# A graph-attention layer and a quantile layer: start-up loads on POOL's queue, shared gather rounds, and the quantile mean on ScalarE and TensorE

## The chip, the cores and the metric

The kernel runs on one core of a Trainium2 chip. The metric is the device time of one execution in microseconds (us). A core has five engines that each work through their own instruction stream in order: TensorE (PE in the profile, its weight loads PEld), VectorE (DVE), ScalarE (ACT), GpSimd (POOL) and SyncE (SP, which here only issues transfers). Engines wait for one another by semaphores. A DMA is issued from the stream of an engine, in order with that engine's other instructions.

## The reference

4096 nodes with 128 features, and a symmetric 4096 x 4096 adjacency matrix with ones on the diagonal, about one entry in 64 set. Layer 0 is graph attention with 8 heads:

```python
Wh = einsum('nd,hde->hne', nodes, W)
f1 = einsum('hnd,hd->hn', Wh, a1); f2 = einsum('hnd,hd->hn', Wh, a2)
e = leaky_relu(f1[:, :, None] + f2[:, None, :], 0.2)
att = softmax(where(adj > 0, e, -9e15), axis=-1)
h = elu(einsum('hnm,hmd->hnd', att, Wh))
x = elu(transpose(h, (1, 0, 2)).reshape(N, 8 * 128) @ W1 + b1)
out = layernorm(nodes + x, gamma, beta)
```

Layer 1 has an adjacency list per node, thinned: of the node's neighbours in order, those whose rank plus one is a multiple of half their number are removed. For each feature, the values of the kept neighbours are sorted, and the values at the ranks of the quantiles 0.25, 0.5 and 0.75 are averaged:

```python
svals = sort(where(keep[:, :, None], x[None], big), axis=1)
for q in (0.25, 0.5, 0.75):
    idx = maximum(ceil(q * n_keep) - 1, 0)
    agg = agg + (1/3) * take_along_axis(svals, idx)
agg = 0.5 * agg + 0.5 * x
out = agg @ W.T + b + x
```

## The kernel before

Line numbers are those of the kernel before, which are also those in its profile. The layers are sparse: neighbours are fetched as rows by indirect DMA (one instruction fetches 128 rows of 512 or 544 bytes, one for each partition, by a list of 128 row numbers). The program (`gnn`) is `gat`, then `sparse`. A second path (`general`) would be taken for graphs that do not fit the sizes assumed, and is not executed here.

**The front (class `Front`).** Nodes are taken in tiles of 128, and tiles in blocks of 4, 4, 6, 6, 6, 6. `scan` loads a tile's adjacency rows in four quarters of 512 KB on SP's queue (three buffers), ACT makes zeros and ones of them (L371, L378), and PE packs 16 columns into a word (L380), into `ps_words`. From the second pair of tiles on, two tiles are scanned together. `first` (L393 and the helper `drain8`, L186 and L188) drains the nonzero words on DVE, 8 a round in 13 rounds; `second` unpacks the bits; another drain puts each node's neighbour list in order. When a block's tiles are through, `place` sorts its nodes by number of neighbours: it computes each node's place in the block (`pos_i`, L509), and 4 or 6 indirect scatters on POOL (L530) write the lists to the DRAM array `rows_d` in that order. `keep` thins the lists for layer 1 (`meta_d`), and after the last block `order` computes each node's place in a global order by number of kept neighbours, which 32 scatters (`scatter`, L669) write to `order_d`. These steps are a list of `pieces`; `advance(n)` puts the next n of them into the program.

**The table.** `table` (L228) loads W, a1, a2 and x, forms W·a for the heads, transposes x on PE, with copies on ACT, and writes a table `xf_d` to DRAM: a row of 128 features, 8 values f2 and 8 values f1 for each node, and a padding row. Twelve DMAs, all from ACT's queue. `gat` then loads the weights, bias, gamma and beta, and writes two padding rows of the table of layer 1, whose source is set by DVE (L817): seven DMAs more from ACT's queue.

**The attention.** The work is cut in 64 units, each half a tile. In a unit, 4 groups of 16 nodes each have an upper bound on their neighbours (nodes being sorted, `BOUNDS` gives it), and a group is fetched in r rounds; in a round, a gather (L890) fetches 8 neighbours for each of the 16 nodes. r is the bound plus 2, over 8, rounded up, so a last round is partly padding. `load(u)` issues these gathers on POOL three units ahead, into six `nb` buffers of 18 rounds. Row numbers come from `ids`, which SP loads from `rows_d` once for a block, with `info`, which the gathers `me` (L866) and the scatters of results (L1098) need. DVE adds f1 and f2 (L966), ACT and DVE form the softmax numerators, DVE spreads them (L1005), and PE multiplies one 128 x 128 matrix per round into `ps_z` (L1012). A framework schedules the instructions of each engine: the order in which they lie in the built program follows dependences and its own estimates, unless `issue_after` ties them, so it is not always the order of the source.

**The quantile stage.** `sparse` (L1570) takes the 32 tiles of the global order. For each it gathers as many rows as the tile's largest list (L1607, POOL; three row buffers), and runs a sorting network over the slots: a step copies the low side on ACT into a PSUM bank or a small buffer (L1645), then DVE takes minimum and maximum (L1650, L1651). Two tiles are interleaved. `quantile` then knows, for each of three quantiles, a short range of sorted slots in which the node's rank lies. DVE forms 0 or 1/3 weights for them (L1684) and sums the weighted slots in `agg`: one L1695 and several L1698 a tile. Where a list is longer than 64, the slots above are merged in by `cut` operations (L1665, L1675, L1680). For a group of up to four tiles, `finish` then has four items: PE adds half of `agg` and half of x, transposed (L1711, L1712); ACT copies that (L1716); PE applies the layer (L1722 to L1724); ACT copies the result (L1728), and POOL scatters it to the output (L1732). Such items wait in a list, from which `compare` takes one a step: a "copy" item after any ACT copy of the network, a "bank" item only in steps with 5 to 12 slots, in the free end of that step's PSUM bank. There are two banks.

## Time and profile before

| | us |
| --- | --- |
| median of 3 runs | 7742.63 (7739.80 to 7743.64) |
| the profiled execution, whole | 7742.94 |
| its span | 7741.1 |
| end of the first block's places (`pos_i`) | 170.2 |
| first neighbour gather | 179.9 |
| first compare of the quantile stage on DVE | 3269 |
| last DVE instruction | 7727.0 |
| mean granted TensorE clock | 0.553 |

The profile is of one execution. Its parts are busy time by engine, the span in 40 slices of 193.5 us with each engine's busy tenths, groups of instructions (line, engine, operation, tiles, shapes and count, then busy time, the mean of one in ns, and the idle time just before them on their engine with what ended it), waits, and a timeline. "issue" in the idle column is time in which an engine waited for nothing that the profile shows. DMA instructions on POOL show the time that POOL spends on them, not that of the transfer.

### The profile page before, as it was taken

The page shows a single profiled execution, that of the slowest core. Times are in us where ns is not written, and L with a number is a line of the kernel's source. Part 1 is how long each engine was busy: PE and PEld are TensorE (multiplying, and loading weights), DVE is VectorE, ACT ScalarE, POOL GpSimd, SP SyncE. Part 2 cuts the span into 40 slices and gives each one's busy share as a digit, 9 for nine tenths or more (in the row PEclk, how much of TensorE's full clock was granted, in tenths as well). Part 3 has the DMA queues.
Part 4 walks back from the last instruction along what each step waited for, and adds up shares of the span by engine and source line. Part 5 has one row for each costly group of instructions (what it writes and reads, how often), then busy time and mean ns, then how long its engine had stood idle before and what let it go on. Part 6 is the DMA issues. An engine that isn't in the chain of part 4 may idle for free. (4 is left out here: it accounts for less than half of the span.)

```text
span 7741.1 us, 30455 instructions
## 1 busy us (share of the span) xinstructions
PE 1051.4 (14%) x5811; PEld 887.8 (11%) x5811; DVE 5841.9 (75%) x9358; ACT 2162.5 (28%) x2127; POOL 4386.7 (57%) x4564
## 2 busy tenths in 40 slices
PE   3233242332232223200000000000000000000000
PEld 1122232222232222100000000000000000000000
DVE  6456465564332222289999999999999999999999
ACT  5021112000000000133333333333333333333332
POOL 0777777777777777575545636354635534554400
PEclk5566666665566666655555555555555555555555
DMA  5232324222222222111111101011101101111100
GB/s 183 67 100 78 97 78 113 64 60 56 47 56 56 56 56 56 41 48 37 35 32 36 42 24 43 27 38 31 45 23 36 36 27 29 37 36 31 31 3 1
DMA packets 222435, 385.05 MB, mean 50 GB/s; under 512 B 121622, under 2 KB 133274, under 8 KB 222234
## 3 DMA queue, kind: packets, MB, share of 16 engines
q0 software_dynamic: 145664, 305.55, 15.4%
q1 hardware_dynamic: 64258, 70.19, 3.0%
q10 hardware_dynamic: 12312, 7.28, 0.3%
q14 instruction: 154, 1.26, 0.1%
q8 instruction: 47, 0.77, 0.0%
HBM read 372.41 MB, written 10.31 MB: 49 GB/s over the span
## 5 line engine op out<-in xcount | busy, mean ns | idle before, releaser
L1607 POOL DMA_INDIRECT rows<-x_d,info x2078 | 2022.4, 973 | 1962.4 <-DVE agg L1698 1272.7
L890 POOL DMA_INDIRECT nb<-xf_d,ids x2250 | 2140.2, 951 | 697.0 <-issue 652.8
L1645 ACT COPY low<-rows 128x2048 f32<-128x2048 f32 (+8 forms) x1022 | 1561.3, 1533 | 2599.7 <-DVE rows L1651 1964.0
L1650 DVE TENSOR_TENSOR rows<-low,rows 128x2048 f32<-128x2048 f32 (+8 forms) x1022 | 1883.1, 1861 | 114.5 <-ACT low L1645 33.8
L1651 DVE TENSOR_TENSOR rows<-low,rows 128x2048 f32<-128x2048 f32 (+8 forms) x1022 | 1881.7, 1860 | 4.7
L966 DVE TENSOR_TENSOR e<-nb,ps_small 128x144 f32<-128x144 f32 (+8 forms) x166 | 43.5, 264 | 1314.1 <-DMA nb<-xf_d,ids 1246.9
L1012 PE MATMUL ps_z<-spread,nb 128*128 128x128 f32 x4500 | 612.1, 304 | 770.2 <-DVE spread L1005 749.0
L1012 PEld LDWEIGHTS ps_z<-spread,nb 128*128 128x128 f32 x4500 | 601.0, 219 | 804.5 <-DVE spread L1005 367.3
L1711 PE MATMUL low<-half_i,agg 128*128 128x128 f32 x64 | 22.2, 451 | 4297.1 <-ACT low L1645 4191.2
L974 ACT ACTIVATE ps_e<-e 128x256 f32<-128x256 f32 (+4 forms) x64 | 26.1, 408 | 1941.1 <-DVE e L966 1856.6
L1711 PEld LDWEIGHTS low<-half_i,agg 128*128 128x128 f32 x64 | 16.9, 325 | 4300.6 <-ACT low L1645 4193.6
L1005 DVE TENSOR_TENSOR spread<-e,ps_small 128x1152 f32<-128x1152 f32 (+4 forms) x312 | 342.9, 1107 | 87.8 <-PE ps_z L1012 85.3
L1732 POOL DMA_INDIRECT out<-o,info x32 | 33.4, 1044 | 383.6 <-ACT o L1728 359.3
L371 ACT ACTIVATE nz<-a_i 128x1024 bf16<-128x1024 int32 x128 | 134.4, 1051 | 229.4 <-DMA a_i<-in_adj 188.5
L1645 ACT COPY low_s<-rows 128x512 f32<-128x512 f32 (+3 forms) x325 | 139.8, 471 | 142.8 <-DVE rows L1650 61.4
L186 DVE MAX8 k<-key 128x8 f32<-128x256 f32 x416 | 165.7, 413 | 0.9
L1650 DVE TENSOR_TENSOR rows<-low_s,rows 128x512 f32<-128x512 f32 (+3 forms) x325 | 158.0, 499 | 2.6 <-ACT low_s L1645 2.1
L1651 DVE TENSOR_TENSOR rows<-low_s,rows 128x512 f32<-128x512 f32 (+3 forms) x325 | 158.7, 499 | 0.3
L188 DVE MATCH_REPLACE8 key<-k,key 128x256 f32<-128x256 f32 x384 | 155.9, 408 | 0.0
L904 DVE TENSOR_TENSOR mine<-me,group 128x64 f32<-128x64 f32 x32 | 6.8, 213 | 196.6 <-DMA me<-xf_d,info 193.5
L380 PE MATMUL ps_words<-nz,pows 128*128 128x512 bf16 (+1 forms) x272 | 109.8, 559 | 291.9 <-ACT nz L378 192.8
L1653 DVE TENSOR_TENSOR rows<-rows 128x256 f32<-128x256 f32 (+8 forms) x245 | 141.4, 579 | 0.2
(227 smaller groups left out, 2584.8 us busy)
## 6 DMA issues: line engine op xcount, KB each, us to landing
a_i<-in_adj SPq DMA_DIRECT2D x128, 512.0 KB, 4.4
nb<-xf_d,ids POOLq DMA_INDIRECT x2250, 2.5
rows<-x_d,info POOLq DMA_INDIRECT x2078, 2.4
xf_d<-xf ACTq DMA_DIRECT2D x4, 576.0 KB
xf<-in_x ACTq DMA_DIRECT2D x4, 512.0 KB
meta_d<-rowdata_k SPq DMA_DIRECT2D x4, 324.0 KB, 4.0
abc_ta<-in_L_gnn_a ACTq DMA_DIRECT2D x2, 512.0 KB, 8.6
w_ga<-in_L_gnn_W ACTq DMA_DIRECT2D x2, 512.0 KB, 4.9
```

The costliest lines, as they stand in the source:

```text
L186: nc.vector.max(out=top, in_=work)
L188: nc.vector.match_replace(out=work, in_to_replace=top, in_values=work, imm_value=gone)
L371: nc.scalar.activation(nz[:, j, :], a_i, AF.Relu, scale=-1.0, accum_out=self.negative[:, k : k + 1],)
L380: nc.tensor.matmul(ps_w[:, :m, :], self.pows[:, 4 * i + b, :], nz[:, :m, ts(b, NG1)], start=i + b == 0, stop=i + b == 6,)
L890: gather = nc.gpsimd.indirect_dma_start(out=rows[:, at + i, :], out_offset=None, in_=xf_d, in_offset=bass.IndirectOffsetOnAxis(ap=ids[:, k ...
L1005: last = nc.vector.tensor_tensor(spread[:, :m], e[:, at : at + m, :].unsqueeze(2).to_broadcast(shape), own.unsqueeze(1).unsqueeze(3).to_br ...
L1012: product = nc.tensor.matmul(ps_z[:, g, :], rows[:, k + i0 + i, :D], spread[:, i].rearrange("p j h -> p (j h)"), start=i0 + i == 0, stop=i ...
L1607: nc.gpsimd.indirect_dma_start(out=row, out_offset=None, in_=x1_d, in_offset=bass.IndirectOffsetOnAxis(ap=info[:, col : col + 1], axis=0),)
L1645: nc.scalar.copy(packed, lows)
L1650: nc.vector.tensor_tensor(lows, packed, highs, op=ALU.min)
L1651: nc.vector.tensor_tensor(highs, packed, highs, op=ALU.max)
L1653: nc.vector.tensor_tensor(lows, lows, highs, op=ALU.min)
```

## The change

Four edits in one:

- The 19 DMAs of `table` and of the start of `gat` go from ACT's queue to POOL's. `table` gets a call in its middle (`between`), which puts the front's next two pieces, `first` of the first two tiles, into the program there, after the loads and before the transposes; the products with a1 and a2 move up behind it. The `first` of a tile that comes after block 0's `place` in the program is tied behind that block's `pos_i`.
- The 32 `order_d` scatters leave the list of pieces; the source puts them into the program at the first unit that has nothing left to load, 61 of 0 to 63.
- In a half tile, the partly filled last rounds of groups can share a gather: `shared_rounds` packs them into rounds of 8 slots. The row numbers of the second and further groups of such a round are loaded from `rows_d` with an offset (`others`), and merged by a maximum into those of the first (padding has number 0). Each group still multiplies the round's rows on PE, and slots of other groups get a large negative logit from `outside`.
- `quantile` makes all weights of a tile in one DVE operation, 0 or 1. The weighted slots are formed on ACT (`scale`), and summed on PE against a sixth of the identity, together with half of x (`sums`); ACT copies the sum to `comT`. So a tile has three waiting items, and `finish` two. `cut` works in pieces of at most 32 slots.

```diff
-def table(tc, nc, c, x, w, a1, a2, xf_d):
+def table(tc, nc, c, x, w, a1, a2, xf_d, between):
...
-        nc.scalar.dma_start(out=w_sb, in_=w.rearrange("h d e -> d h e"))
...
+        nc.gpsimd.dma_start(out=w_sb, in_=w.rearrange("h d e -> d h e"))
+        wa = tp.tile([P, 2 * H], F32, name="wa_ta")
+        abcs = []
+        for a in (a2, a1):
+            abc = tp.tile([P, H, D], F32, name="abc_ta", bufs=2)
+            nc.gpsimd.dma_start(
+                out=abc.rearrange("p h e -> p (h e)"),
+                in_=a.rearrange("h e -> (h e)").partition_broadcast(P),
+            )
+            abcs.append(abc)
         xf = tp.tile([P, NT, XF], F32, name="xf")
         for i in range(4):
-            nc.scalar.dma_start(
+            nc.gpsimd.dma_start(
                 out=xf[:, ts(i, 8), :D],
                 in_=x[ts(i, 1024), :].rearrange("(t p) d -> p t d", p=P),
             )
+        nc.gpsimd.dma_start(out=xf_d[0:1, :], in_=pad)
+        between()
+        for i, abc in enumerate(abcs):
+            nc.vector.tensor_mul(abc, abc, w_sb)
+            nc.vector.reduce_sum(wa[:, ts(i, H)], abc, axis=AX.X)
...
         for i in range(4):
-            nc.scalar.dma_start(
+            nc.gpsimd.dma_start(
                 out=xf_d[1 + i * 1024 : 1 + (i + 1) * 1024, :].rearrange(
...
-        nc.vector.tensor_copy(pos_i, pos)
+        placed = nc.vector.tensor_copy(pos_i, pos)
+        if b == 0:
+            self.placed = placed.ins
...
-                        self.first(t, bufs["k1"][:, j, :])
+                        with ExitStack() as order:
+                            if self.placed is not None:
+                                order.enter_context(self.tc.issue_after(self.placed))
+                            self.first(t, bufs["k1"][:, j, :])
...
-        for t in range(NT):
-            out.append((None, lambda t=t: self.scatter(t, state["pos"], order_d)))
-        return out
+        late = [lambda t=t: self.scatter(t, state["pos"], order_d) for t in range(NT)]
+        return out, late
+
+
+def shared_rounds(most):
+    bins = []
+    for n, g in sorted(((h % SL, g) for g, h in enumerate(most)), key=lambda v: (-v[0], v[1])):
+        for members in bins if n else []:
+            used = sum(k for _, k in members)
+            if used + n <= SL:
+                members.append((g, n))
+                break
+        else:
+            if n:
+                bins.append([(g, n)])
+    out = {}
+    for members in bins:
+        at = 0
+        for g, n in sorted(members):
+            if len(members) > 1:
+                out[g] = min(members)[0], at, n
+            at += n
+    return out
...
-        table(tc, nc, c, x, w, a1, a2, xf_d)
+        table(tc, nc, c, x, w, a1, a2, xf_d, lambda: advance(2))
...
-        nc.scalar.dma_start(out=w_sb, in_=w.rearrange("h d e -> d h e"))
+        nc.gpsimd.dma_start(out=w_sb, in_=w.rearrange("h d e -> d h e"))
...
+        for i, (at, n) in enumerate(spans):
+            to = outside[:, i : i + 1]
+            nc.vector.tensor_scalar(
+                to, slot[:, :1], float(at), -4.0 * BIG, op0=ALU.is_lt, op1=ALU.mult
+            )
+            nc.vector.tensor_scalar(
+                slot[:, 1:], slot[:, :1], float(at + n), -4.0 * BIG, op0=ALU.is_ge, op1=ALU.mult
+            )
+            nc.vector.tensor_add(to, to, slot[:, 1:])
...
+            for i, (t, g, _, at) in enumerate(joined):
+                nc.sync.dma_start(
+                    out=others[:, i : i + 1],
+                    in_=dram_view(
+                        rows_d,
+                        t * P * ROW + part * (P * g - at) + rounds(t, g) - 1,
+                        [[part, P], [1, 1]],
+                    ),
+                )
+            for i, (t, _, g, _) in enumerate(joined):
+                k = first[t] + g * tops[t] + rounds(t, g) - 1
+                to = ids[:, k : k + 1]
+                nc.vector.tensor_tensor(to, to, others[:, i : i + 1], op=ALU.max)
...
+                own_ = r[g] - (v is not None and v[0] != g)
...
+                if own_ < r[g]:
+                    where[-1].append(where[v[0]][-1])
+                    gathers[u][g, own_] = gathers[u][v[0], r[v[0]] - 1]
...
+                if whole < r[g]:
+                    rows, k = where[g][-1]
+                    i = spans.index(shared[u][g][1:])
+                    nc.vector.scalar_tensor_tensor(
+                        e[:, at + whole, :],
+                        rows[:, k, D:],
+                        outside[:, i : i + 1],
+                        f1[:, g, :],
+                        op0=ALU.add,
+                        op1=ALU.add,
+                    )
...
             if u + 3 < 2 * NT:
                 held[u + 3] = load(u + 3)
+            elif late:
+
+                advance(len(todo))
+                for piece in late:
+                    piece()
+                late = []
...
+        sixth = one.tile([P, P], F32, name="sixth_i")
+        nc.scalar.mul(sixth, c["idf"], 0.5 * float(np.float32(1.0 / NQ)))
...
+            nc.vector.tensor_tensor(
+                weight[:, :, : last - first + 1],
+                iota_p[:, first + shift : last + 1 + shift].unsqueeze(1).to_broadcast(shape),
+                info.bitcast(F32)[:, POS : POS + NQ].unsqueeze(2).to_broadcast(shape),
+                op=ALU.is_equal,
+            )
...
-                for i in range(n):
-                    v = view(rows, lo - 1 + i)
-                    if not begun:
-                        nc.vector.tensor_scalar(agg, v, weight[:, i : i + 1], None, op0=ALU.mult)
-                        begun = True
-                    else:
-                        nc.vector.scalar_tensor_tensor(
-                            agg, v, weight[:, i : i + 1], agg, op0=ALU.mult, op1=ALU.add
-                        )
...
+            def scale():
+                made["v"] = tp.tile([P, MOST, D], F32, name="picked", bufs=1)
+                for i, (v, weight) in enumerate(found):
+                    nc.scalar.mul(made["v"][:, i, :], v, weight)
+
+            def sums(ps):
+                made["ps"] = ps[:, :P]
+                for i in range(len(found)):
+                    nc.tensor.matmul(
+                        made["ps"], made["v"][:, i, :], sixth, start=i == 0, stop=False
+                    )
+                nc.tensor.matmul(made["ps"], x1, half, start=False, stop=True)
+
+            return [
+                ("copy", scale),
+                ("bank", sums),
+                ("copy", lambda: nc.scalar.copy(comT, made["ps"])),
+            ]
...
-            return [("bank", halves_), ("copy", half_copy), ("bank", layer), ("copy", layer_copy)]
+            return [("bank", layer), ("copy", layer_copy)]
```

## The prediction

> **What bounds the kernel now.** I read the page's parts 1 and 2 first, then the groups of POOL and DVE, windows by stage, the timeline of the front, and the waits of the last stage.
>
> ```profile
> PE 1051.4 (14%) x5811; PEld 887.8 (11%) x5811; DVE 5841.9 (75%) x9358; ACT 2162.5 (28%) x2127; POOL 4386.7 (57%) x4564
> ...
> DVE  6456465564332222289999999999999999999999
> ...
> POOL 0777777777777777575545636354635534554400
> ```
>
> DVE has 75% of the span, but the slices split it: in the first 16 or so (193.5 us each) it is 20 to 60% busy while POOL stands at 7, then DVE goes to 9 and POOL falls. So there are three stages: a front until POOL's first gather, a GAT stage until about 3200 us, and the quantile stage. Windows (span, then busy time of PE, PEld, DVE, ACT, POOL, clock, DMA share, GB/s) in the second and third:
>
> ```profile
> 180.00:700.00 520.00, 145.14 (x838) 120.78 (x837) 284.77 (x1266) 86.81 (x139) 393.68 (x415) 0.62 0.34 89
> ...
> 3400.00:5000.00 1600.00, 34.78 (x120) 27.73 (x120) 1570.02 (x1273) 619.50 (x476) 836.68 (x865) 0.50 0.13 36
> ```
>
> In the GAT stage nothing but POOL is near its limit, and its missing quarter is issue time, as the groups of POOL show (busy, mean ns, idle before and what ended it):
>
> ```profile
> L890 POOL DMA_INDIRECT nb<-xf_d,ids x2250 | 2140.2, 951 | 697.0 <-issue 652.8 <-DMA nb<-xf_d,ids 19.8 <-PE ps_z L1012 8.6
> L1607 POOL DMA_INDIRECT rows<-x_d,info x2078 | 2022.4, 973 | 1962.4 <-DVE agg L1698 1272.7 <-issue 614.7 <-DVE weight L1684 65.2
> ...
> L530 POOL DMA_INDIRECT rows_d<-rowdata,pos_i x32 | 31.2, 976 | 176.0 <-DVE pos_i L509 166.6 <-issue 8.5 <-DVE pos_g L647 0.3
> L669 POOL DMA_INDIRECT order_d<-node,pos_g x32 | 31.0, 969 | 9.8 <-issue 8.8 <-DVE s L1092 0.3 <-DMA order_d<-node,pos_g 0.3
> ```
>
> A gather costs (2140.2+652.8)/2250 = 1.24 us of the span, back to back: POOL bounds this stage. In the quantile stage DVE is 98% busy (1570 of 1600) and POOL waits for it. Before 170 us POOL waits 166.6 us for `pos_i`, so DVE's chain to `pos_i` bounds the front. Its gaps (timeline: start, length, idle before):
>
> ```profile
> 61.61 0.31 DVE L817 MEMSET pad<- 1x128 f32 x2 [21.95 <-DMA xf_d<-xf]
> ...
> 67.92 0.42 DVE L393 SCALAR_TENSOR_TENSOR key<-ps_words,iota_g 128x256 f32<-128x256 f32 x1 [5.33 <-PE ps_words L380]
> ...
> 87.91 0.75 DVE L393 SCALAR_TENSOR_TENSOR key<-ps_words,iota_g 128x256 f32<-128x256 f32 x2 [7.30 <-PE ps_words L380]
> ```
>
> **The change, part by part.**
>
> **Gathers shared.** From the bounds on the degrees, the last rounds that fit together save 8 gathers of 283 in a block of four tiles and 11 of 421 in one of six: 2×8+4×11 = 60, so 2190 remain. At 1.24 to 1.25 us each: −75 (−70 if some of the 28 us that POOL waits otherwise grow, −78 with these gone). Products on PE stay 4500. Added: 60 `others` loads on SP, 60 DVE maxima of 128×1 on the ids, some 115 masks of 128×8. DVE has 235 of 520 us free in the window above, more later, which hides 175 ops of 0.2 to 0.25 us (about 40 us); with that cover gone they would cost those 40. At the start they are on the path: `info`, which the row gather `me` needs, stands on SP behind 8 `others`, and the seventh gather needs a maximum. Gathers before it take 6×1.25 us and the ids come as before, so I take +1 (0 to +5, five such loads' worth of issue gaps). In later blocks they wait behind rows_d scatters, tens of us before use.
>
> **Late scatters.** The 32 `order_d` scatters cost 32 × (0.969+0.3) = 40.8 us of POOL's path. The source puts them after the last gathers, but in the order of the built program they still stand in mid-stream, after gather 1297 of 2190 (before: 1333 of 2250): they depend only on `order`, and the scheduler pulls them forward. So 0; if they did move into the quantile stage, where POOL is idle, −40.
>
> **Early first block.** 19 plain DMAs go from ACT's queue to POOL's, ahead of the rows_d scatters; 11 of them have 1024 pieces. ACT, which scans, no longer waits in order for them. Now DVE: tile 0 had its words at 20.4 us; two tiles' scan is eight loads of 512 KB, about 19.5 us, so tiles 2 and 3 can have theirs near 50, against 87.9 seen. The built order on DVE is the two `abc` products (4.85 us, which fit in the 16 us that DVE idles first), tiles 0 and 1 (13 us each; tile 1 took 67.9 to 80.6), the pair 2/3 (18.6: 87.9 to 106.5), with the pad memsets in its middle. From there to `pos_i` took 63.6 us, of which some 17 net were keys of tiles 4 and on, which now wait for `pos_i`: 47 remain. 50+18.6+47, and 4 for the span set-up, is 120 instead of 170: −50. That is one end, where a plain DMA on POOL costs what a gather costs, 0.95. No row shows one; the other end is a gather's price per piece, 128 rows in 0.95, so 7.6 us for 1024. Then w_ta, both abc and four xf keep POOL until 43, the copy into xf and four stores until 85, and the memsets, which wait for the stores as they did in the row of 21.95 above, hold DVE some 20 us; late xf also holds ACT's transposed copies between scan steps, about 8: `pos_i` at 148, −22, and −15 with the first gather's own tables late. A regular pattern needs no id per row, so it is nearer to the first end in kind, but eight times the pieces: I take `pos_i` at 135, −35. What is late next is DVE itself. Holding back tiles 4 and on delays block 1: its scatters stood 60 us behind its `pos_i` on POOL (369.7 against 429); after, I put this at 38, so it is hidden.
>
> The rule that speaks against this is in the Trainium skill, "DMA: Bandwidth & Descriptors", section "SWDGE vs HWDGE vs iDMA": plain transfers belong on SP or ACT, because on GpSimd software writes each descriptor. Another, "SBUF — State Buffer", section "SBUF: two separate sides", says that such a DMA of 620 ns alone took 3100 ns beside a VectorE copy in its two-port mode; five times 0.95 would be an estimate of 4.8 us each and a gain near 28. The gathers here are 951 ns beside a half-busy DVE and 973 beside a 98% busy one, which shows no such factor for this mix of operations.
>
> **Quantile mean.** The rows of DVE in the last stage that go, and its waits (us in total, times, longest):
>
> ```profile
> L1698 DVE SCALAR_TENSOR_TENSOR agg<-rows,weight,agg 128x128 f32<-128x128 f32 x118 | 40.2, 341 | 0.8
> ...
> L1684 DVE TENSOR_SCALAR weight<-iota_p,info 128x1 f32<-128x1 f32 x61 | 12.3, 203 | 0.0
> ...
> L1695 DVE TENSOR_SCALAR agg<-rows,weight 128x128 f32<-128x128 f32 x32 | 8.8, 274 | 0.2
> ```
>
> ```profile
> DVE rows L1650 <- ACT low L1645: 33.8, 43, 1.9
> ...
> DVE rows L1650 <- PE low L1724: 22.1, 7, 5.5
> ...
> DVE rows L1650 <- PE low L1712: 2.5, 4, 1.3
> ```
>
> 40.2 + 8.8 + 20.1 (all 96 of L1684) is 69 us of busy time, but neighbours overlap (two MAX8 of 0.43 take 0.74), 246 × 0.09 = 22: 47 net. Added on DVE: 32 weight operations of 78 to 153 columns, between the rows of 203 and 274 ns, net 0.18: +5.8; six more `cut` pieces: +0.5. PE takes 182 matmuls into borrowed banks: L1712's waits give 0.3 us for an 8-matmul item, 32 items +10 at most, less the 2.5 that go: I take +5. ACT takes 150 multiplications of 0.28 and 32 copies; it waits for DVE 1964 us in this stage, which hides them; but four of them ahead of a copy that DVE needs cost 1.1 us a tile, 0 to 35, and the 43 waits above say that ACT is rarely the late one: +8. They stand in ACT's built order within a few copies of each quantile, so `rows` is freed before POOL's slack (1272.7/31, about 41 us a tile) is used up. The tail: 13 operations of DVE took 4.99 us; instead 14 ACT products and 15 PE matmuls of 0.42 to 0.56 (6.3 to 8.4) run in a row: +2 (0 to +4). Sum −47+5.8+0.5+5+8+2 = −26 (−46 to +8).
>
> **Sum.** −75+1+0−35−26 = −135. The profiled execution took 7742.94 us (span 7741.1 and 1.8 around it), 0.3 above the median, so 7742.9−135 = 7608.
>
> **Rivals.**
> - POOL's plain DMAs cost a gather's price per piece: front −15 rather than −35, 7628. For: only per-row prices are in the trace. Against: regular patterns. 0.17.
> - The quantile's gain is taken by ACT and PE waits: 0 instead of −26, 7634. For: L1724's 5.5 us shows a bank can be held long. Against: ACT's slack. 0.12.
> - The full gains, or scatters that do land late (another −40): 7568 to 7590. 0.07.
> - Slower: a plain DMA on POOL is slower by far than any row. Without the front's −35 the rest gives −100, and a loss of over 115 is needed, so `pos_i` near 285: 11 DMAs of 24 us or more, three times the upper end. For: nothing but that no row shows one. 0.07.
> - Within 0.2% (15 us, about what can be told from no change here): the same with some 20 us each, 0.03.
>
> **How the numbers follow.** The forecast has 0.54 (7590 to 7625). The range sums the ends: −50−78−46 = −174 gives 7569, −15−70+5+8 = −72 gives 7671, widened to 7567 and 7685 because two of the costs have no row at all; above it lies about 0.1. Faster 0.90, same 0.03, slower 0.07.
>
> **What would show it.** `pos_i` ending at 120 to 148 and DVE's 21.95 gap gone; 2190 gathers at an unchanged 1.25 us period and a GAT stage 75 shorter; order_d scatters still amid the gathers; in the quantile stage DVE some 40 us less busy, its waits for ACT `low` and PE `low` together under 75 (58 now), POOL still waiting for DVE or ACT there. I am wrong if POOL's plain DMAs take over 8 us each, if POOL shows new waits for the ids at block starts, or if DVE's waits for ACT `low` double.

## The result and the profile after

The changed kernel took 7646.99 us (median of 4 runs, 7646.79 to 7647.49) against 7741.75 us of the kernel before on the same chip (4 runs, 7739.80 to 7743.64): a ratio of 0.9878, with a 95% interval of 0.9861 to 0.9895, or 94.8 us less. The forecast was 7608, 135 less, with a range of 7567 to 7685. The profiled execution took 7646.96 us, its span 7645.2.

Line numbers from here on are those of the changed kernel. The page's parts 1 and 2 after:

```profile
PE 1122.8 (15%) x6047; PEld 946.8 (12%) x6047; DVE 5831.7 (76%) x9380; ACT 2214.1 (29%) x2301; POOL 4343.5 (57%) x4524
...
DVE  8465555565223222399999999999999999999999
...
POOL 2777677777777777565554645455536434554500
```

The shape is the same: a front, a stage in which POOL stands at 7, a stage in which DVE stands at 9. POOL's first slice is 2 where it was 0: it now holds the 19 plain DMAs, and the gathers start 37 us earlier in it. Three points of the timeline cut the span into stages: the first neighbour gather on POOL, the first compare on DVE with a copy from ACT, and the last output scatter on POOL.

| | before | after | difference | forecast |
| --- | --- | --- | --- | --- |
| start to first gather | 179.9 | 142.5 | −37.4 | −34 |
| gathers: to first compare | 3089.4 | 3044.5 | −44.8 | −75 |
| quantiles: to last output scatter | 4461.5 | 4454.2 | −7.3 | −26 |
| last scatter to the end | 10.4 | 3.9 | −6.5 | 0 |
| span | 7741.1 | 7645.2 | −95.9 | −135 |

No cause was found for the last row but one. In the variants of the changed kernel below, this stretch took between 3.9 and 8.3 us, also with the old quantile mean (3.9), and in run 12, the kernel before with three info buffers, 10.1 us. Nothing in the prediction bears on it.

**The front.** POOL's timeline in the first 145 us (start, length, idle before):

```profile
5.17 3.54 POOL L253 DMA_DIRECT2D xf<-in_x  x4
...
56.17 3.57 POOL L269 DMA_DIRECT2D xf_d<-xf  x4 [46.94 <-ACT xf L267]
...
133.25 1.04 POOL L541 DMA_INDIRECT rows_d<-rowdata,pos_i  x1 [57.96 <-DVE pos_i L518]
...
142.51 0.99 POOL L971 DMA_INDIRECT nb<-xf_d,ids  x1 [4.40 <-DMA ids<-rows_d]
```

Here is the price that no row of before had: a plain DMA of 1024 pieces takes POOL 3.54/4 = 0.89 us, a little less than a gather of 128 rows, and not eight times as much. The four loads, issued while DVE stood idle (until 10.99 below), and the four stores, issued beside DVE's drain of the keys of tiles 2 and 3, cost the same, 3.54 and 3.57 us. The Trainium skill ("SBUF — State Buffer", section "SBUF: two separate sides") warns that a DMA issued by GpSimd waits for its descriptors while VectorE runs an operation in its two-port mode, a copy for instance. No such delay shows here, but that drain is not a copy, so no row here tests the case of the warning. On DVE the keys of the tiles 2 and 3 start at 52 us instead of 88, and of the 21.95 us of idle time before the pad memset 7 are left:

```profile
10.99 1.22 DVE L260 TENSOR_TENSOR abc_ta<-abc_ta,w_ta 128x1024 f32<-128x1024 f32 x1 [6.51 <-DMA abc_ta<-in_L_gnn_a]
...
52.07 0.76 DVE L402 SCALAR_TENSOR_TENSOR key<-ps_words,iota_g 128x256 f32<-128x256 f32 x2 [6.98 <-PE ps_words L389]
...
70.60 0.30 DVE L856 MEMSET pad<- 1x128 f32 x2 [7.04 <-ACT nz L380]
...
132.79 0.17 DVE L518 CAST pos_i<-pos 128x4 int32<-128x4 f32 x1
```

**The gathers.** Groups of POOL over the whole span:

```profile
L971 POOL DMA_INDIRECT nb<-xf_d,ids x2190 | 2086.0, 953 | 707.0 <-issue 632.2 <-PE ps_z L1111 36.9 <-DMA nb<-xf_d,ids 22.2
...
L1197 POOL DMA_INDIRECT x_d<-s,info x32 | 31.4, 982 | 68.6 <-DVE s L1194 44.8 <-DMA x_d<-s,info 14.7 <-issue 6.1
...
L680 POOL DMA_INDIRECT order_d<-node,pos_g x32 | 30.8, 962 | 9.8 <-issue 8.8 <-DMA order_d<-node,pos_g 0.6 <-DVE e L1063 0.3
```

There are 60 gathers less, at an unchanged 951 to 953 ns and 0.3 of issue: (2140.2+652.8) − (2086.0+632.2) = 74.8 us, the 75 of the forecast. But POOL now waits 36.9 us for `ps_z`, that is for PE to free a gather buffer, where it waited 8.6. That is 28.3 of the missing 30. The 32 scatters of `order_d` cost what they cost before.

Most of the new wait stands at one place, the start of block 2, with 30.1 us where the kernel before had 7.2. In POOL's timeline there:

```profile
819.66 0.94 POOL L971 DMA_INDIRECT nb<-xf_d,ids  x1 [8.49 <-PE ps_z L1111]
...
849.19 0.97 POOL L1197 DMA_INDIRECT x_d<-s,info  x1 [1.53 <-DMA x_d<-s,info]
...
854.34 0.98 POOL L947 DMA_INDIRECT me<-xf_d,info  x1 [4.18 <-DMA info<-rows_d]
...
883.19 0.94 POOL L971 DMA_INDIRECT nb<-xf_d,ids  x1 [21.61 <-PE ps_z L1111]
```

SP's transfers at the same time, SP's wait ahead of the load of `info` (from SP's waits between 690 and 905: us in total, times, longest), and then DVE:

```profile
783.08 5.75 SPq L919 DMA_DIRECT2D others<-rows_d  x11
...
851.49 0.38 SPq L932 DMA_DIRECT2D info<-rows_d  x1
```

```profile
SPq L932 <- DMA x_d<-s,info: 42.7, 1, 42.7
```

```profile
799.18 0.46 DVE L1074 TENSOR_TENSOR ps_e<-e,ps_e 128x288 f32<-128x288 f32 x1 [39.36 <-ACT ps_e L1073]
...
860.09 0.23 DVE L989 TENSOR_TENSOR mine<-me,group 128x64 f32<-128x64 f32 x1 [17.28 <-DMA me<-xf_d,info]
...
861.50 0.58 DVE L188 MAX8 lists<-cand 128x8 f32<-128x176 f32 x2
...
875.33 0.82 DVE L1103 TENSOR_TENSOR spread<-e,ps_small 128x640 f32<-128x640 f32 x1
```

Read together: SP waits 42.7 us with the load of `info` until POOL has scattered results of block 0, which it does at 849; SP loads `info` at 851, POOL can then gather `me` at 854, DVE stands still for 17 us until that lands at 860, then a drain of the scan (13.9 us of DVE) lies ahead of the next spread at 875. PE multiplies behind it, and only then has POOL a free buffer, at 883. The kernel before went through the same steps, with less behind them:

```profile
894.25 0.38 SPq L851 DMA_DIRECT2D info<-rows_d  x1
```

```profile
896.99 0.99 POOL L866 DMA_INDIRECT me<-xf_d,info  x1 [4.09 <-DMA info<-rows_d]
...
911.48 0.94 POOL L890 DMA_INDIRECT nb<-xf_d,ids  x1 [7.24 <-PE ps_z L1012]
```

Farther up in the changed kernel, DVE idles 39 us for a softmax step of ACT, which stood in ACT's queue behind scan steps that waited for their adjacency load:

```profile
793.18 1.06 ACT L380 ACTIVATE nz<-a_i 128x1024 bf16<-128x1024 int32 x1 [71.77 <-DMA a_i<-in_adj]
```

**The quantiles.** DVE's waits in this stage (us in total, times, longest), and the group of the new products on ACT:

```profile
DVE rows L1756 <- ACT low L1751: 50.0, 52, 1.9
...
DVE rows L1756 <- PE low L1837: 20.3, 8, 3.3
...
DVE rows L1756 <- PE low L1818: 12.3, 10, 2.2
```

```profile
L1810 ACT ACTIVATE picked<-rows,weight 128x128 f32<-128x128 f32 x150 | 52.1, 393 | 94.6 <-DVE rows L1797 81.6 <-DVE rows L1757 6.7 <-DVE rows L1761 3.7
```

The stretch from the first compare to the last one, before and after (length, then busy time of PE, PEld, DVE, ACT and POOL, granted clock, DMA share, GB/s):

```profile
3269.20:7722.10 4452.90, 91.46 (x310) 71.98 (x310) 4349.37 (x3583) 1700.72 (x1362) 2101.28 (x2154) 0.50 0.11 32
```

```profile
3187.00:7632.90 4445.90, 148.32 (x524) 119.55 (x524) 4316.02 (x3389) 1751.27 (x1527) 2098.03 (x2154) 0.50 0.11 32
```

It fell by 7 us. DVE is busy there for 4316.0 us instead of 4349.4: the edit did take 33 us off. But the waits for ACT's copies rose from 33.8 to 50.0, and those for PE's use of the banks from 24.6 to 32.6, and with some smaller ones 26 of the 33 went back.

### The profile page after: what moved, and what is told of

It is laid out like the page before. It is cut to its first block, busy times and chain, and to the rows that moved or that the text cites. A ratio compares the mean times of both kernels' runs of the same rounds, so it can differ in the third digit from the quotient of the medians.

```text
span 7645.2 us, 31290 instructions
## 1 busy us (share of the span) xinstructions
PE 1122.8 (15%) x6047; PEld 946.8 (12%) x6047; DVE 5831.7 (76%) x9380; ACT 2214.1 (29%) x2301; POOL 4343.5 (57%) x4524
## 5 line engine op out<-in xcount | busy, mean ns | idle before, releaser
L971 POOL DMA_INDIRECT nb<-xf_d,ids x2190 | 2086.0, 953 | 707.0 <-issue 632.2
L1756 DVE TENSOR_TENSOR rows<-low,rows 128x2048 f32<-128x2048 f32 (+9 forms) x1022 | 1884.7, 1862 | 138.9 <-ACT low L1751 50.0
L1757 DVE TENSOR_TENSOR rows<-low,rows 128x2048 f32<-128x2048 f32 (+9 forms) x1022 | 1882.4, 1861 | 5.8
L1054 DVE TENSOR_TENSOR e<-nb,ps_small 128x64 f32<-128x64 f32 (+9 forms) x200 | 47.7, 240 | 1252.6 <-DMA nb<-xf_d,ids 1206.7
L1815 PE MATMUL low<-sixth_i,picked 128*128 128x128 f32 x300 | 79.8, 442 | 4224.7 <-ACT low L1751 3736.4
L1815 PEld LDWEIGHTS low<-sixth_i,picked 128*128 128x128 f32 x300 | 66.8, 324 | 4237.7 <-ACT low L1751 3744.8
L1751 ACT COPY low_s<-rows 128x512 f32<-128x512 f32 (+3 forms) x325 | 139.8, 471 | 130.5 <-DVE rows L1756 48.0
L1757 DVE TENSOR_TENSOR rows<-low_s,rows 128x512 f32<-128x512 f32 (+3 forms) x325 | 158.7, 500 | 0.3
L190 DVE MATCH_REPLACE8 key<-k,key 128x256 f32<-128x256 f32 x384 | 155.5, 407 | 0.0
L1142 PE MATMUL ps_h<-zT,w_ga 128*128 128x256 f32 x256 | 116.3, 619 | 198.4 <-DVE s L1414 106.6
```

The source lines that it names most:

```text
L190: nc.vector.match_replace(out=work, in_to_replace=top, in_values=work, imm_value=gone)
L971: gather = nc.gpsimd.indirect_dma_start(out=rows[:, used + i, :], out_offset=None, in_=xf_d, in_offset=bass.IndirectOffsetOnAxis(ap=ids[:, ...
L1751: nc.scalar.copy(packed, lows)
L1756: nc.vector.tensor_tensor(lows, packed, highs, op=ALU.min)
L1757: nc.vector.tensor_tensor(highs, packed, highs, op=ALU.max)
L1815: nc.tensor.matmul(made["ps"], made["v"][:, i, :], sixth, start=i == 0, stop=False)
```

## The experiments

Twelve kernels ran in four groups, each group on one chip and beside runs of the kernel before there, which took 7742.1, 7749.7, 7742.0 and 8501.9 us. So times of different groups are compared by their ratio to before, or by the stages. Where nothing was edited, the time to the first gather (141.2 to 143.6 us) and the quantile stage (4454.2 to 4455.5) agree within 2.5 us. The stage of the gathers lies between 3044.5 and 3046.5, but is 3050.6 in run 7, where a gather cost POOL 955 ns instead of 953, 5.7 us over 2190 of them. The changed kernel's own ratio is 0.9878.

| run | ratio (95% interval) | median, us | first gather | gathers | quantiles | POOL waits for ps_z |
| --- | --- | --- | --- | --- | --- | --- |
| changed kernel | 0.9878 (0.9861 to 0.9895) | 7647.0 | 142.5 | 3044.5 | 4454.2 | 36.9 |
| 1 scan loads on ACT's queue | 0.9889 (0.9874 to 0.9904) | 7656.0 | 153.2 | 3039.8 | 4454.6 | 39.0 |
| 2 no shared rounds | 0.9939 (0.9926 to 0.9953) | 7695.0 | 139.8 | 3087.6 | 4454.9 | 8.0 |
| 3 old quantile mean | 0.9884 (0.9869 to 0.9899) | 7654.3 | 143.6 | 3046.5 | 4462.5 | 38.0 |
| 4 table DMAs on ACT | 0.9879 (0.9863 to 0.9894) | 7649.7 | 146.0 | 3042.1 | 4455.2 | 37.2 |
| 5 three info buffers | 0.9846 (0.9832 to 0.9859) | 7628.5 | 143.4 | 3018.5 | 4454.5 | 18.0 |
| 6 scatters really late | 0.9826 (0.9812 to 0.9839) | 7613.2 | 141.7 | 3004.5 | 4455.5 | 37.5 |
| 7 products one by one | 0.9882 (0.9867 to 0.9897) | 7657.1 | 141.5 | 3050.6 | 4457.0 | 36.1 |
| 8 no tie on tiles 4 and on | 0.9887 (0.9872 to 0.9902) | 7662.6 | 155.5 | 3046.5 | 4454.7 | 38.3 |
| 9 products on POOL | 0.9892 (0.9877 to 0.9907) | 7658.2 | 142.5 | 3046.5 | 4464.6 | 39.9 |
| 10 edits 5 and 6 | 0.9798 (0.9784 to 0.9811) | 7585.4 | 143.1 | 2981.5 | 4454.8 | 18.9 |
| 11 edits 5, 6 and 9 | 0.9809 (0.9796 to 0.9823) | 7593.9 | 141.2 | 2979.9 | 4465.2 | 15.0 |

The twelfth stands at the end, by itself.

**1. The scan's loads on another queue.** My first theory for the 28 us was SP's order.

```diff
-                nc.sync.dma_start(out=a_i, in_=self.adj[ts(t + j, P), ts(i, quarter)])
+                nc.scalar.dma_start(out=a_i, in_=self.adj[ts(t + j, P), ts(i, quarter)])
```

> The changed kernel, with one edit: the adjacency loads of the scan are issued from ACT's queue instead of SP's. Theory A: in the changed kernel SP is stuck in order. The row lists of block 2 (ids, the new others, info) wait on SP for scatters that stand in POOL's stream, the scan's loads wait behind them, ACT waits 71.8 us for such a load with a softmax step queued behind it, DVE idles 39.4 us for that step, and POOL then waits for buffers (36.9 us for ps_z in all, 8.6 in the kernel before). With the scan's loads on another queue POOL's waits for ps_z fall to 10 or less and the time falls by 20 to 30 us, to about 7620. Theory B: DVE has too much of its own work at the start of block 2, because the keys of tiles 4 and on are held back; then POOL still waits about 37 us and the time stays within 10 us of 7647.

The wait for `ps_z` stayed (39.0), and the time did not fall. ACT's timeline shows that the edit did not set the loads free:

```profile
795.24 6.00 ACTq L378 DMA_DIRECT2D a_i<-in_adj  x3
801.29 1.06 ACT L380 ACTIVATE nz<-a_i 128x1024 bf16<-128x1024 int32 x1 [68.02 <-DMA others<-rows_d]
```

The loads, now in ACT's stream, waited for `others` there. In this run's trace the transfers of SP and ACT tell of their landing by the same eight semaphores, and each waits first for the earlier transfer that used its own: the load of the scan at 795.24 uses the semaphore of a load of `ids` that SP issued at 791.73. So the scan still depended on block 2's lists, and the run does not tell theory A from B. It shows one thing more: with these loads on ACT's queue the first gather came 10.7 us later.

**2. No shared rounds.**

```diff
-        shared.append(shared_rounds(most))
+        shared.append({})
...
-        spans = sorted({v[1:] for half in shared for v in half.values()})
+        spans = [(0, SL)]
```

> The changed kernel without shared rounds: 2250 gathers again, no others loads, no maxima, no masks. 60 gathers at 1.25 us bring 75 us back. Theory A, that the others loads (5.75 us on SP for block 2, ahead of the scan's load) and the merged rounds make POOL's new waits for ps_z: those waits fall back to about 9 us, so the net is 75 - 28 = +47, about 7694. Theory B, that the waits come from the late keys of block 1 and 2: the 28 us stay and the time rises by the full 75, to about 7722.

The time is 7695.0, one us from theory A's number, and the wait for `ps_z` is back at 8.0 us. So the part is worth 43 us in its stage (3087.6 − 3044.5), not 75, and the new wait comes with it and not with the late keys alone. That the time agrees to 1 us is in part chance: of the 45.5 us by which the span is longer than the changed kernel's, 4.4 lie after the last scatter. The same place in this run's DVE timeline:

```profile
858.34 0.27 DVE L989 TENSOR_TENSOR mine<-me,group 128x64 f32<-128x64 f32 x1 [18.21 <-DMA me<-xf_d,info]
...
863.64 0.82 DVE L1103 TENSOR_TENSOR spread<-e,ps_small 128x640 f32<-128x640 f32 x1
```

DVE stands for `me` here too, 18.2 us. But the spread comes 5.3 us after it, and not 15.2, because this program's order on DVE has the drain elsewhere. So the shared rounds moved the points at which the waits meet; that they load an engine more is not what these rows show.

**3. The old quantile mean.** `quantile`, `finish` and the group's tiles as in the kernel before; everything else as changed.

```diff
...
-                found = quantile(t - 1, *held.pop(t - 1), plans[t - 1][2])
-                waiting += pick(found, xs[:, at, :], comT[:, at, :])
+                agg = group[first][1]
+                quantile(t - 1, *held.pop(t - 1), plans[t - 1][2], agg[:, t - 1 - first, :])
...
```

> The changed kernel with the quantile mean of the kernel before (weights, weighted sums and old cut on DVE, halves on PE). From the stages of the two profiles, the quantile part gave 7 us in its body and 6.7 in its tail: +14 us, about 7661. DVE's waits for ACT low fall from 50 to about 34 and for PE low from 32.6 to about 25. If the quantile stage of the changed kernel gained by anything else than this part, or if the part also cost in the stage before, the time differs from that by more than 8 us.

The quantile stage is 8.3 us longer (4462.5), the median 7.3. The waits went as expected, to 33.8 for ACT and 24.2 for PE. The 14 us that I expected were too many: 6.5 of them were the time after the last scatter, which is short here as well (3.9 us). The part is worth 7 to 8 us.

**4. The table's DMAs back on ACT's queue.**

```diff
-        nc.gpsimd.dma_start(out=w_sb, in_=w.rearrange("h d e -> d h e"))
+        nc.scalar.dma_start(out=w_sb, in_=w.rearrange("h d e -> d h e"))
```

and so for the other 18.

> The changed kernel with its 19 plain DMAs back on ACT's queue; the early keys of tiles 0 and 1 and the holding back of tiles 4 and on stay. Theory A: the queue matters, because ACT waited in order for tables (14.7 us and 10.2 us in the kernel before) with the scan behind it: pos_i ends 10 to 25 us later than 132, and the time rises by as much. Theory B: only the order of DVE's work matters, and the time stays within 5 us.

Theory B holds: the first gather comes 3.5 us later and the time is within 3. The queue, which looked like the heart of this part, matters little here.

**5. Three info buffers.** The ring that the timelines show can be opened by a buffer.

```diff
-            info = tp.tile([P, max(BLOCKS), 2], I32, name="info")
+            info = tp.tile([P, max(BLOCKS), 2], I32, name="info", bufs=3)
```

> The changed kernel with three buffers instead of two for info (the node lists that block by block SP loads after ids and others). Theory A: of the 36.9 us that POOL waits for ps_z, 21.6 stand at the start of block 2 and come from a ring through four queues: the load of info waits on SP for its buffer until the results of block 0 are scattered (849 us), me waits on POOL for info (854), DVE stands from 843 to 860 us for me, and the next spread, which frees a buffer, comes at 875. With a third buffer info loads with the lists, me does not wait, POOL's waits for ps_z fall to about 16 us and the time falls by 15 to 22 us, to about 7628. Theory B: DVE's own queue is the cause, a drain of 14 us of the scan of later tiles in front of that spread; then DVE is late without me too and less than 7 us are gained.

Theory A holds, and by more: the stage is 26.0 us shorter. `info` follows the lists at once, and the wait that was 21.61 is now 9.70 (SP, then POOL):

```profile
789.80 0.43 SPq L932 DMA_DIRECT2D info<-rows_d  x1
```

```profile
792.66 0.94 POOL L947 DMA_INDIRECT me<-xf_d,info  x1 [4.24 <-DMA info<-rows_d]
...
865.36 0.98 POOL L971 DMA_INDIRECT nb<-xf_d,ids  x1 [9.70 <-PE ps_z L1111]
```

18.9 us of the 26.0 are in the wait for `ps_z` (36.9 to 18.0), and 8.1 in the wait of `me` for `info` (12.3 to 4.2). The gathers' waits named `DMA nb` fell too, from 22.2 to 7.6, but those named "issue" grew from 632.2 to 647.1: together they are the same 0.3 us before a gather, under two names. DVE's long stand for the softmax step is still there, so the 26 us did not hang on it:

```profile
798.77 0.46 DVE L1074 TENSOR_TENSOR ps_e<-e,ps_e 128x288 f32<-128x288 f32 x1 [38.50 <-ACT ps_e L1073]
```

What the remaining 9.70 us wait for is open.

**6. Scatters that are really late.** The last gather of the last unit is named, and the scatters are tied to it.

```diff
+                last = gathers[2 * NT - 1][HALF - 1, halves_[2 * NT - 1][0][-1] - 2]
+                with ExitStack() as order:
+                    order.enter_context(tc.issue_after(last))
-                for piece in late:
-                    piece()
+                    for piece in late:
+                        piece()
```

> The changed kernel, with the 32 order_d scatters tied behind the last gathers, so that they really come where the source puts them. They are 40 us of POOL. POOL waits 40.1 us for the last results (x_d) at that place, so they should fit into that hole: GAT stage 35 to 40 us shorter, 7607 to 7612. Rival: the loads of order on SP, and with them the first gathers of the quantile stage, come after the last scatter, and the hole is shorter by the time that the scatters land; then the gain is under 30.

The stage is 40.0 us shorter, so the rival falls. The wait for the last results in the changed kernel, and then POOL's timeline of this run at the same place:

```profile
3146.65 0.98 POOL L1197 DMA_INDIRECT x_d<-s,info  x1 [40.09 <-DVE s L1194]
```

```profile
3064.72 0.94 POOL L971 DMA_INDIRECT nb<-xf_d,ids  x1 [0.30 <-issue]
3065.97 0.99 POOL L680 DMA_INDIRECT order_d<-node,pos_g  x1 [0.30 <-issue]
...
3105.15 1.08 POOL L680 DMA_INDIRECT order_d<-node,pos_g  x1 [0.31 <-issue]
3106.53 0.95 POOL L1197 DMA_INDIRECT x_d<-s,info  x1 [0.30 <-issue]
```

The 32 scatters fill exactly the 40 us in which POOL waited for the last results, and the scatter of these follows without a wait. So what the change says of the scatters is worth 40 us, and the change does not do it.

**7. Products one by one.**

```diff
-                ("copy", scale),
+                *[("copy", lambda i=i: scale(i)) for i in range(len(found))],
...
-                nc.scalar.copy(packed, lows)
+                copied = nc.scalar.copy(packed, lows)
                 if waiting and waiting[0][0] == "copy":
-                    waiting.pop(0)[1]()
+                    with tc.issue_after(copied.ins):
+                        waiting.pop(0)[1]()
```

> The changed kernel with the products of the quantile mean as single items, each tied behind its own copy of the network, instead of two to four in a row on ACT. Theory A: the 16 us that DVE waits more for ACT low come from the copies held up by rows of two to four products (0.3 us each); spread out, that wait falls from 50 to 40 or less, and the time by 5 to 12 us. Theory B: any product in front of a copy that DVE needs costs its 0.3 us, in a row or not; the wait stays at 45 to 55 and the time within 4 us.

Theory A falls: the wait for ACT `low` is 52.0, the stage 2.8 us longer. Their standing in a row is not the cause. Whether it is their presence on ACT, run 9 asks. (Of the 7.8 us by which the profiled span is longer, 6.0 are in the gathers, which the edit does not touch.)

**8. No tie.** The condition of the tie is made false.

```diff
-                            if self.placed is not None:
+                            if False:
```

> The changed kernel without the tie that holds the keys of tiles 4 and on behind pos_i of block 0. Theory A: of the 37 us by which the first gather came earlier, about 17 are these keys, so pos_i ends 12 to 18 us later than 132. The time then rises by 12 to 18 us, if nothing later is helped by early keys, to about 7662. Theory B: the tie does nothing for pos_i because the words of those tiles are not there before; time within 5 us.

The first gather comes at 155.5, 13.0 us later, and the later stages do not change by more than 2. Theory A holds for the front. POOL waits 38.3 us for `ps_z` here too, without the late keys; with run 2 this shows that the late keys neither bring this wait nor are needed for it. (The ratios, 0.9887 against 0.9878, agree with 13 us, but their intervals are as wide.)

**9. Products on POOL.**

```diff
-                    nc.scalar.mul(made["v"][:, i, :], v, weight)
+                    nc.gpsimd.tensor_scalar(made["v"][:, i, :], v, weight, None, op0=ALU.mult)
```

> The changed kernel with the products of the quantile mean on POOL instead of ACT. Theory A: DVE's wait for ACT low rose from 33.8 to 50 because these products add work to ACT's in-order queue, whether in a row or spread out. Without them on ACT it falls back to about 34, the quantile stage (first compare to the last output scatter, 4454 us) is 10 to 16 us shorter, and so is the time. Rival: products on POOL (no run has shown one yet) come after row gathers in POOL's queue or slow DVE's compares; then PE's sums come late, or the mean of the compares rises, and the stage is as long as with ACT or longer.

The rival holds. The stage is 10.4 us longer. POOL takes nearly twice ACT's 393 ns for one:

```profile
L1810 POOL TENSOR_SCALAR picked<-rows,weight 128x128 f32<-128x128 f32 x150 | 113.0, 761 | 1558.5 <-DVE rows L1797 976.4 <-DVE rows L1756 292.4 <-DVE rows L1761 174.0
```

DVE's waits in this stage:

```profile
DVE rows L1756 <- ACT low L1751: 41.6, 43, 1.9
...
DVE rows L1756 <- PE low L1818: 16.7, 14, 2.6
...
DVE weight L1769 <- POOL picked L1810: 11.2, 8, 2.2
```

The wait for ACT `low` fell to 41.6, half of the way back. So the products' presence on ACT accounts for about half of what was added there, and the cause of the other half is open; the copies to `comT`, 32 now where there were 9, stay on ACT in this run and were not tested. The waits for PE `low` L1818 rose to 16.7, DVE's next weights wait 11.2 us for the products, and the tail, in which 14 of these run in a row, is 1.5 us longer (from the last compare's end to the last output scatter 9.9 us, against 8.4).

**10 and 11. Together.** Number 10 has the edits of 5 and 6, number 11 that of 9 too.

> The changed kernel with three info buffers and with the scatters tied behind the last gathers. If the 26 us and the 40 us that the stage of the gathers lost with the one and the other have nothing to do with each other, it falls from 3044 to about 2979 us, and the time to about 7581. If less than 60 us are gained, they shared a wait.

> Both edits of the run before and the products on POOL: the sum, about 7567 if the products gain 14 us there, and as slow as the run before or slower if they do not.

Number 10 gains 63.0 us in the stage of the gathers, of 26.0 + 40.0, and takes 7585.4 us: 2.0% less than the kernel before, and 0.8% less than the changed one. It beats both. Number 11 is 8.5 us slower than 10, as 9 foretold.

**12. The kernel before, with three info buffers.**

> The kernel before the change with three info buffers and nothing else. There POOL waited only 7.2 us for ps_z at the start of block 2 and 4.1 us for info. Theory A, that the ring was there already but had slack, and the shared rounds used it up: 5 to 12 us are gained, against the 26 us that the same edit gave in the stage of the gathers of the changed kernel. Theory B, that the ring cost as much before, hidden under other names: about 26 us are gained here too.

This run says nothing on it. On the chip that it got, the kernel before itself took 8501.9 us, the edited one 8520.1 (ratio 1.0018, 1.0008 to 1.0027), and its profile shows waits that no other run has: 337.5 us of POOL for `ps_z`, 247.4 us for events called remote. Whether the ring cost the kernel before anything is open.

## Why the prediction was right or wrong

The sign, the range and the order of the parts were right: 7647 lies inside, and faster had 0.90. The size was 40 us too large, from two terms. That it was not more is in part luck: 6 us came after the last scatter, where nothing was forecast and no cause is known.

- **What bounds each stage**: right for the first two. Keys of later tiles that could again run ahead of `pos_i` on DVE lengthened the front by 13.0 us (run 8). Removing POOL's gathers shortened the stage of the gathers, undoing it (run 2) lengthened it, and the scatters moved into POOL's idle time shortened it by their full length (run 6). In the quantile stage DVE is busy 97% of the time, but 33 us less of its work gave only 7.
- **Front, −35**: −37.4. `pos_i` ended at 133.0, forecast 135. The chosen middle was right, for a reason that was not: plain DMAs on POOL cost 0.89 us, the low end, which should have given 120. Of the 13 us between 120 and 133.0, 2 are the words of tiles 2 and 3, which came at 52 and not 50; 7.0 are DVE's stand before the memset of `pad`, for which that end had nothing; and about 4 the keys of tiles 4 and on, worth 13.0 in run 8 where the prediction took 17. By runs 4 and 8, the queue gave 3.5 us of it and the tie 13.0; the remaining 21 is what the early first two tiles leave, by subtraction and not by a run. The rival that a price per piece makes POOL's DMAs slow is refuted.
- **`others` at the start, +1**: no sign of it; the seventh gather follows the sixth after 0.3 us. Setting up the masks, for which the front's sum has 4 ("the span set-up"), took 26 operations and 3.7 us of DVE; without nearly all of them (run 2) the first gather came at 139.8, 2.7 us earlier.
- **Gathers, −75**: the 74.8 us of POOL's time went away, but the stage fell by 44.8. The step that failed is "In later blocks they wait behind rows_d scatters, tens of us before use", with which all effects on later blocks were costed at nothing; the prediction allowed 5 us (−70) if POOL's 28 us of other waits grew. The wait for `ps_z` alone grew by 28.3 us. It is a wait for buffers and came from a ring of SP, POOL, DVE and PE at block 2 in which the kernel before had 7 us of waiting. Run 2 shows that the shared rounds bring the wait, run 5 that opening the ring at `info` takes 18.9 us of it away and 26.0 of the 30 us that the stage had lost. By which of its instructions the part tipped the ring is not settled: `others` hold SP for 5.75 us there, and the order on DVE differs too.
- **Late scatters, 0**: right; the order of the built program told it. Run 6 shows that the 40 us given for the other case were right as well.
- **Quantile mean, −26**: −7.3. DVE's work fell by 33.4 us in the stretch between the first and the last compare, where the forecast has 47 − 6.3, less the 5 of the tail: 36. The sum counts the tail's 4.99 us twice: they are in the 47 (its 13 operations are among the 246), and again in the +2, which is 6.3 to 8.4 less these 4.99. Counted once, the terms give −21. (The range's lower end, −46, is also lower than the terms' own ends, which give about −43.) The mis-sized terms are the +8 for ACT, which measured 16.2, and the +5 for PE, which measured 8.0; smaller waits added 2. The products took 52.1 us in all, 0.35 each and not 0.28. "ACT is rarely the late one" was read from the 43 waits of the kernel before, and "which hides them" from the 1964 us that ACT waits for DVE, a sum over the stage: with the change there were 52 waits. The products seldom stand right in front of a late copy: at 48 of the 52, with 45.7 of the 50.0 us, ACT had itself last waited for DVE's step before it (L1757). How they delay it is not shown. The tail measured −0.3 instead of +2. The rival "taken by ACT and PE waits" is nearer to what happened than the forecast: it gave 0, and 19 of the forecast's 26 us did not come, 5 of them for the double count.

The missing 39 us of the span are these two, 30 and 19, less 3 for the front and `others` and 6 after the last scatter.

## What to carry to other kernels

A gain on the engine that bounds a stage is whole only as far as its buffers keep up: look at each place where that engine already waited a little for another one (7 us for `ps_z`, 4 us for `info`), follow that wait back through all queues, and count such places as having no slack until a run shows some. An engine's slack over a stage says little when work is added into an in-order queue that another engine reads step by step, and neither does the number of its present waits: 1964 us of slack and 43 waits (33.8 us) became 52 waits (50.0 us). Where a term is a difference of old and new work, see that the old work is not also taken off in another term. And where a scheduler decides the order, an edit of the source's order may be no edit: compare the orders of the built programs, then tie what must be late to what it must follow, and see whether POOL, or whichever engine it is, has a hole of that length.

## What the runs showed of the hardware

- A plain DMA issued by POOL took it 0.5 to 0.57 us with few pieces and 0.89 to 1.10 us with 1024; the first one was the longest (1104 ns). Four with DVE idle took 3.54 us, four beside DVE's drain 3.57.
- A product of 128x128 with one scalar per partition took 393 ns on ACT and 761 ns on POOL, while a copy of that size on ACT took 294 (low_s) or 264 ns (from PSUM). In a row they overlap: twelve on ACT took 3.61 us, fourteen on POOL 8.14.
- In the tail 24 matmul instructions of 128x128 (two for each product) took PE 5.24 us, 0.22 each, with no gap between them; two at a time, with waits between, took 0.80. The granted clock at both places was 0.5 in the profile's slices.
